# Two tensors in one room of SBUF, 64 or 128 bytes apart: a GNN kernel on one core

## The chip, the core and the metric

The kernel runs on one core of a Trainium2 chip. The metric is the time on the device in microseconds (us) of one execution of the whole program; of several runs the median is given. A profile of one execution shows when each instruction of each engine began and ended.

## The reference

The input x has 64 graphs of 256 nodes with 512 features, in 32-bit floats; adj is one 256 x 256 matrix of zeros and ones that all graphs share. Two layers follow one another, each on a layer norm with a ReLU, and each added to its input:

```python
# layer 0
h = relu(layernorm(x))
q, k, v = h @ Wq.T, h @ Wk.T, h @ Wv.T
rel = adj.T * (q @ k.T)                    # per graph, 256 x 256
rel = rel / norm(rel, axis=2)
x = x + rel @ v
# layer 1
h = relu(layernorm(x))
x = x + (adj @ h) @ weight + bias
```

## The kernel before

The work goes by pairs of graphs: 32 pairs, 512 rows each, one after the other. Since q and k are used only in their product, the kernel works out M = Wq.T Wk once, and per pair g = M h and the scores g.T h. Each 32-bit factor of a product is split into an upper part (u), a lower part (l) and a sum-like third part (s), and three matmuls in a reduced 32-bit format (fp32r) stand for one exact product. So most rooms come as three, named _u, _l and _s.

The stages of a pair that TensorE works on, with the shape of the moving operand:

- g_stage: g = M h, 48 matmuls of 512 columns (stationary m_p, moving h). `split_right_ps` (ACT L265, DVE L266, DVE L268) writes the three parts of g from PSUM into the rooms gy_u, gy_s and gy_l.
- v_stage: v = h Wv, 48 matmuls of 512 columns (stationary h, moving wv_p).
- scores: 48 matmuls of 256 columns. The stationary operand is a 128 x 128 block of g, another one for every matmul; the moving operand is h of one graph, 256 columns.
- attend: rel times v, 24 matmuls of 512 columns.
- gather: adj times the second layer's h, for the pair before, 32 matmuls of 256 columns. The stationary operand is a block of v_low or late_parts, the moving one is the turned adjacency, adjt. `split_left_ps` (ACT L274, DVE L275, L276) writes the three parts of the result, y, into the rooms gy_u, gy_l and gy_s.
- mix: y times the second layer's weight, 48 matmuls of 512 columns (stationary y, moving w_p).

Nearly all matmuls are recorded at one line, L255, the helper `mm`; the profile tells them apart by the names of their operands, the moving one first: `bank<-h_u,gy_u` with 256 columns are scores, `bank<-w_u,gy_u` with 512 are mix, `bank<-adjt_r,late_parts` are gather.

g and y share the three gy rooms in turn: g is written and read by the scores, then y is written and read by mix, then the next pair's g. They don't start at the same byte. A room holds 4 x 512 floats and BEHIND floats more; y starts at its beginning and g BEHIND floats behind:

```python
BEHIND = 16
def as_y(tile):
    return tile[:, : DC * T].rearrange("p (d t) -> p d t", d=DC)
def as_g(tile):
    return tile[:, BEHIND : BEHIND + DC * T].rearrange("p (d t) -> p d t", d=DC)
```

adjt has an offset too: it lies 112 floats (448 bytes) into its room. Rooms are laid out one after the other along each partition, in the order in which they are first declared. Small ones between the large ones (statistics of the layer norms, row norms, two single columns) and the room named level, which nothing uses, set where the large ones begin.

The order of instructions on each engine isn't written out by hand. A planner (`Plan`) takes each step with its engine, an assumed cost and the keys that it reads and writes, simulates the engines, and issues the steps in the order of their simulated starts. Keys are names such as ("gy_u", d, half), not addresses. Because g lies a little behind y, the writing of a block of y also names the end of the block of g that it overlaps, by ("g_u", d - 1, 1) or ("g_u", d, 0).

A program compiled for both cases of the adjacency picks, at run time, the branch for one whose values are exact in the reduced format; this input takes that branch.

Of the kernel before, what the change touches and what calls it, by code (L numbers as in the profile page):

```python
# [113 lines left out]
def kernel(  # L114
# [15 lines left out]
    NC = N // P  # L130
    NB = 2
# [11 lines left out]
    def room(name, *shape, dtype=F32, tag=None):  # L143
        return pool.tile([P, *shape], dtype, name=name, tag=tag or name)

    def parts_room(name, *shape, tag=None):
        return [room(f"{name}_{k}", *shape, dtype=F32R, tag=f"{tag or name}_{k}") for k in "uls"]
# [16 lines left out]

    BEHIND = 16
    w_p = parts_room("w", DC, D)

    def as_y(tile):  # L170
# [5 lines that stand above are left out]
    def norm_rooms(j):  # L176
        return [(room(f"st{j}{n}", TC, 6), room(f"mv{j}{n}", TC, 2), room(f"rs{j}{n}", TC), room(f"nb{j}{n}", TC))
                for n in range(2)]
    wq_room = room("wq_sb", DC * T + BEHIND, tag="gy_u")
    stats = [norm_rooms(0)]  # L180
    norms = [room(f"rn{n}", NB, NC) for n in range(2)]
    wk_room = room("wk_sb", DC * T + BEHIND, tag="gy_l")
    stats.append(norm_rooms(1))
    ones, low_max = room("ones", 1), room("low_max", 1)
    gy_s = room("gy_s", DC * T + BEHIND, dtype=F32R)
    wq_sb, wk_sb = as_y(wq_room), as_y(wk_room)
    low_any = pool.tile([1, 1], I32, name="low_any")
    bias_bc = room("bias_bc", D)
    ident = room("ident", P)
    wq_last, wk_last = room("wq_last", D), room("wk_last", D)  # L190
    room("level", 104)

    rooms = {}

# [427 lines left out]
    def before_pairs():  # L622
        A.activation(norms[1][:, 0, 0:1], ones, AF.Sqrt)
        for _ in range(8):
            mm(bank[7][:, :P], warm, warm, True)
        V.tensor_single_scalar(low, adj_low[:, 0].bitcast(I32), 0xFFF, op=ALU.bitwise_and)
        V.tensor_reduce(low_max, low, axis=mybir.AxisListType.X, op=ALU.max)
        m_products(0)
        mm(bank[7][0:1, 0:1], low_max, ones, True)
        V.tensor_copy(low_any, bank[7][0:1, 0:1])  # L630
        for m in range(NC):
            for n in range(NC):
                nc.tensor.transpose(bank[6][:, ts(m * NC + n, P)], adj_sb[:, n, ts(m, P)], ident)
        for e in range(1, DC - 1):
            m_products(e)
        plan = Plan()
        h_rows(plan, 0, ring[0], "x0")
        plan.run()

    with tc.manual_schedule(engines=in_order):  # L640
        before_pairs()
    gy = [*(room(f"gy_{k}", DC * T + BEHIND, dtype=F32R) for k in "ul"), gy_s]
    g_p, y_p = [as_g(part) for part in gy], [as_y(part) for part in gy]
# [152 lines left out]
```

## Time and profile before

| what | value |
|---|---|
| median of 3 runs | 1561.38 us (1560.41 to 1562.69) |
| the profiled execution's own time | 1560.76 us |
| its span, first to last instruction | 1559.0 us |
| TensorE matmuls | 8046, busy for 1548.2 us |
| TensorE weight loads | busy for 1323.5 us |
| DVE, ACT, GpSimd busy | 1355.3, 1022.7 and 24.3 us |
| granted TensorE clock | 0.999 |

PE in the profile is TensorE's matmuls and PEld its weight loads, which overlap them. A matmul's length in the profile runs from its start to its modelled end, and the next one starts before that end; so the pace is read from one start to the next. In a line of the timeline stand the start in us from the span's start, the length of the merged piece, the engine, the line, the operation, output<-inputs, the shape, and how many instructions were merged.

### The profile page before, as it was taken

What the parts mean: (1) busy time and instruction counts of PE and PEld (TensorE: products, weight loads), DVE (VectorE), ACT (ScalarE), POOL (GpSimd) and SP (SyncE); (2) the same over time, 40 slices, a digit from 0 to 9 for tenths busy, and PEclk for the clock granted to TensorE, in tenths of its full rate; (3) what the DMA queues carried; (4) which work ended last, traced back from release to release, by engine and by line L of the source; (5) the groups of instructions that cost most, each with busy time, mean ns of one, the idle gap of its engine ahead of it and who ended that gap; (6) DMA issues with size and microseconds to landing.
All of it is one profiled execution on the core that took longest, in us unless ns stands there. A gap on an engine that the chain in (4) does not pass through costs nothing.

```text
span 1559.0 us, 22543 instructions
## 1 busy us (share of the span) xinstructions
PE 1548.2 (99%) x8046; PEld 1323.5 (85%) x8046; DVE 1355.3 (87%) x2419; ACT 1022.7 (66%) x1941; POOL 24.3 (2%) x39
## 2 busy tenths in 40 slices
PE   9999999999999999999999999999999999999998
PEld 6788888888888888888888888888888888888886
DVE  6997889898889988898988899888989888989786
ACT  5567666666667676666676675766666766666654
POOL 0000000000000000000000000000000000000000
PEclk9999999999999999999999999999999999999999
DMA  5321333223333223333233332233332233322211
GB/s 199 112 83 41 122 111 120 77 71 110 118 113 119 66 78 117 114 117 90 72 96 118 112 122 68 77 114 114 116 106 71 81 121 111 120 71 76 85 55 56
DMA packets 91112, 153.63 MB, mean 99 GB/s; under 512 B 17136, under 2 KB 32240, under 8 KB 90992
## 3 DMA queue, kind: packets, MB, share of 16 engines
q1 hardware_dynamic: 80768, 116.46, 24.7%
q0 software_dynamic: 8432, 32.51, 5.7%
q10 hardware_dynamic: 1792, 3.15, 0.6%
q8 instruction: 65, 1.06, 0.3%
q14 instruction: 55, 0.45, 0.1%
HBM read 70.78 MB, written 33.55 MB: 67 GB/s over the span
## 4 chain that ended last, share of the span: by engine, by line
PE 95%; DVE 3%; DMA 1%; ACT 0%; issue 0%; ACTq 0%; DVEq 0%
PE bank L255 95%; DMA bias_bc<-in_L_gnn_bias_dram 1%; DMA x_ring<-in_x_dram 1%; DVE late_parts L266 0%; DVE late_parts L268 0%; DVE rel_s_parts L470 0%; DVE st L292 0%; DVE rel_l L475 0%; DVE gy_l L275 0%; DVE m_l L268 0%; DVE gy_l L268 0%; DVE wv_l L268 0%; DVE ht L322 0%; DVE wv_s L266 0%; DVE m_s L266 0%
## 5 line engine op out<-in xcount | busy, mean ns | idle before, releaser
L361 ACT ACTIVATE bank<-bank 128x512 f32<-128x512 f32 x572 | 333.5, 583 | 307.8 <-PE bank L255 304.2
L255 PE MATMUL bank<-wv_s,hs 128*128 128x512 f32 x512 | 137.8, 391 | 0.0
L255 PE MATMUL bank<-wv_u,h_u 128*128 128x512 f32 x512 | 137.5, 390 | 0.0
L255 PE MATMUL bank<-wv_l,h_l 128*128 128x512 f32 x512 | 136.9, 389 | 0.0
L255 PE MATMUL bank<-w_u,gy_u 128*128 128x512 f32 x512 | 136.9, 389 | 0.0
L255 PE MATMUL bank<-w_l,gy_l 128*128 128x512 f32 x512 | 136.9, 389 | 0.0
L255 PE MATMUL bank<-h_l,m_l 128*128 128x512 f32 x512 | 136.6, 389 | 0.1
L255 PE MATMUL bank<-w_s,gy_s 128*128 128x512 f32 x512 | 136.7, 389 | 0.0
L255 PE MATMUL bank<-h_u,m_u 128*128 128x512 f32 x512 | 136.5, 389 | 0.0
L255 PE MATMUL bank<-hs,m_s 128*128 128x512 f32 x512 | 136.4, 389 | 0.0
L266 DVE SCALAR_TENSOR_TENSOR gy_s<-gy_u,bank 128x512 fp32r<-128x512 f32 x128 | 86.2, 675 | 43.0 <-ACT gy_u L265 43.0
L255 PEld LDWEIGHTS bank<-h_l,m_l 128*128 128x128 f32 x512 | 96.0, 188 | 20.4 <-DVE h_l L339 0.5
L255 PEld LDWEIGHTS bank<-wv_l,h_l 128*128 128x128 f32 x512 | 96.1, 188 | 20.2
L255 PEld LDWEIGHTS bank<-h_u,m_u 128*128 128x128 f32 x512 | 96.0, 188 | 20.2 <-ACT m_u L265 0.2
L255 PEld LDWEIGHTS bank<-w_l,gy_l 128*128 128x128 f32 x512 | 96.1, 188 | 20.0
L255 PEld LDWEIGHTS bank<-hs,m_s 128*128 128x128 f32 x512 | 96.1, 188 | 19.9
L255 PEld LDWEIGHTS bank<-w_u,gy_u 128*128 128x128 f32 x512 | 96.0, 188 | 20.0
L255 PEld LDWEIGHTS bank<-w_s,gy_s 128*128 128x128 f32 x512 | 96.0, 188 | 20.0 <-ACT bank L361 0.2
L255 PE MATMUL bank<-adjt_r,late_parts 128*128 128x256 f32 x896 | 112.6, 277 | 0.0
L255 PEld LDWEIGHTS bank<-wv_s,hs 128*128 128x128 f32 x512 | 93.8, 188 | 18.3 <-ACT bank L361 0.7
L255 PEld LDWEIGHTS bank<-wv_u,h_u 128*128 128x128 f32 x512 | 93.7, 188 | 17.7
L255 PEld LDWEIGHTS bank<-adjt_r,late_parts 128*128 128x128 f32 x896 | 107.3, 188 | 0.0
(110 smaller groups left out, 3072.3 us busy)
## 6 DMA issues: line engine op xcount, KB each, us to landing
fresh<-in_x_dram SPq DMA_DIRECT2D x31, 1024.0 KB, 5.7
blocks<-h_rel SPq DMA_DIRECT2D x496, 64.0 KB, 2.0
x_ring<-in_x_dram SPq DMA_DIRECT2D x31, 1024.0 KB, 8.0
out_dram<-x_ring POOLq DMA_DIRECT2D x31, 1024.0 KB, 5.4
h_rel<-h_rel SPq DMA_DIRECT2D x464, 32.0 KB, 1.8
blocks<-in_L_gnn_Wv_dram ACTq DMA_DIRECT2D x1, 1024.0 KB, 11.1
x_ring<-in_L_gnn_weight_dram SPq DMA_DIRECT2D x1, 1024.0 KB, 12.3
out_dram<-x_ring SPq DMA_DIRECT2D x4, 256.0 KB, 2.3
```

Source lines behind the costliest of these rows:

```text
L255: nc.tensor.matmul(out, left, right, start=first, stop=True, skip_group_check=True)
L266: plan.add("DVE", 0.63, lambda: V.scalar_tensor_tensor(s(), f(u()), ONE, ps, op0=ALU.mult, op1=ALU.subtract), [*key, *ku], ks)
L361: plan.add("ACT", 0.49, lambda: A.activation(ps, ps, AF.Copy, scale=ONE), [], [key])
```

## The change

BEHIND goes from 16 to 32 floats, so that g starts 128 bytes behind y in place of 64, and each of the three gy rooms is 64 bytes longer. The small rooms rn0, rn1, ones and low_max, which lay between the large ones, are declared behind the third of them; with that the three gy rooms begin where they began. level shrinks by 48 floats, so that the rooms after it begin where they began. low_any, bias_bc, ident, wq_last and wk_last lie 192 bytes further on.

```diff
-    BEHIND = 16
+    BEHIND = 32
...
     wq_room = room("wq_sb", DC * T + BEHIND, tag="gy_u")
     stats = [norm_rooms(0)]
-    norms = [room(f"rn{n}", NB, NC) for n in range(2)]
     wk_room = room("wk_sb", DC * T + BEHIND, tag="gy_l")
     stats.append(norm_rooms(1))
-    ones, low_max = room("ones", 1), room("low_max", 1)
     gy_s = room("gy_s", DC * T + BEHIND, dtype=F32R)
     wq_sb, wk_sb = as_y(wq_room), as_y(wk_room)
+    norms = [room(f"rn{n}", NB, NC) for n in range(2)]
+    ones, low_max = room("ones", 1), room("low_max", 1)
     low_any = pool.tile([1, 1], I32, name="low_any")
     bias_bc = room("bias_bc", D)
     ident = room("ident", P)
     wq_last, wk_last = room("wq_last", D), room("wk_last", D)
-    room("level", 104)
+    room("level", 56)
```

## The prediction

> **What bounds the kernel now.** I read the profile page first (busy shares, then the chain that ended last), then TensorE's waits, then TensorE's instructions in order of time. The page:
>
> ```profile
> span 1559.0 us, 22543 instructions
> PE 1548.2 (99%) x8046; PEld 1323.5 (85%) x8046; DVE 1355.3 (87%) x2419; ACT 1022.7 (66%) x1941; POOL 24.3 (2%) x39
> PEclk9999999999999999999999999999999999999999
> PE 95%; DVE 3%; DMA 1%; ACT 0%; issue 0%; ACTq 0%; DVEq 0%
> ```
>
> TensorE carries 95% of the chain at an undisturbed clock, and its waits name five single instances that sum to 4.6 us. So the time is the sum of TensorE's own pitches, from one matmul's start to the next one's. A busy time can't show a pitch, because matmuls overlap in the pipeline; starts in the timeline can. One pair in the middle, TensorE alone (start, length, what, how many):
>
> ```profile
> 556.64 1.09 PE L255 MATMUL bank<-wv_s,hs 128*128 128x512 f32 x4
> 557.57 1.11 PE L255 MATMUL bank<-h_u,gy_u 128*128 128x256 f32 x8
> 558.51 1.10 PE L255 MATMUL bank<-h_l,gy_l 128*128 128x256 f32 x8
> 559.45 1.11 PE L255 MATMUL bank<-hs,gy_s 128*128 128x256 f32 x8
> 560.39 0.40 PE L255 MATMUL bank<-adjt_r,v_low 128*128 128x256 f32 x2
> ...
> 562.50 2.66 PE L255 MATMUL bank<-adjt_r,late_parts 128*128 128x256 f32 x22
> 565.00 1.08 PE L255 MATMUL bank<-wv_u,h_u 128*128 128x512 f32 x4
> ```
>
> The scores (moving h, stationary g) take 560.39 - 557.57 = 2.82 us for 24, 117.5 ns each; over all instances the trace gives 117.7. The gather, of the same shape (moving adjt, stationary late rows), takes 2.50 us for 22, 113.6 ns, and 113.3 once settled. A 512-column matmul takes 226.7 ns in steady state, just twice 113.3. So the scores pay 4.4 ns each above a floor that their own shape reaches elsewhere. No engine is waited for, and the clock is the same. Now an early pair:
>
> ```profile
> 130.60 1.07 PE L255 MATMUL bank<-h_u,gy_u 128*128 128x256 f32 x8
> 131.50 1.07 PE L255 MATMUL bank<-h_l,gy_l 128*128 128x256 f32 x8
> 132.41 1.07 PE L255 MATMUL bank<-hs,gy_s 128*128 128x256 f32 x8
> 133.32 0.40 PE L255 MATMUL bank<-adjt_r,v_low 128*128 128x256 f32 x2
> ```
>
> Here the same 24 score matmuls at the same addresses take 2.72 us, 113.3 ns, and the gather that follows in this pair is the slow one, at 118 ns. So there is something like a step between TensorE's two operand streams that persists over hundreds of matmuls, is re-drawn by a disturbance (a 512-column matmul that took 260 ns came just before this pair), and suits either the scores or the gather. Nearly all pairs are of the first kind.
>
> **The addresses.** Laid out from the declared sizes, small rooms rounded up to 32 bytes, and taken modulo 512 bytes: every large room, and so every moving operand of the scores and of all 512-column groups, starts at 128; so do y and nearly all other stationary blocks; adjt starts at 64; g at 192. Scores are thus stationary 192 over moving 128 (64 ahead), the gather 128 over 64 (64 ahead too), everything else 128 over 128. After the change g is at 256, 128 ahead of its moving operand; y does not move, since 64 bytes more of room replace the 64 bytes of small rooms that stood between.
>
> **The change part by part.** No instruction is added, removed or reordered, and no wait: the hand-made schedule works from costs and keys, which are untouched, and y and g overlap in the same blocks as before (the spill of one block into the next grows from 16 to 32 columns of 512, within the same half).
>
> The writes of g (ACT L265, DVE L266 and L268, 128 each) land 64 bytes further. DVE takes 675 ns for gy_s against 668 for the same form into the late rows, which lie at 128: an address costs it under 10 ns, 384 x 10 ns = 3.8 us at most over the span. TensorE hides that: it waits for these engines 2.5 us in all. If that cover were gone, the 3.8 us would be the price. I take 0. The small rooms, bias_bc (L354, 589 ns x128), ident (44 transposes) and wq_last/wk_last (8 matmuls) also move, the four by 192 bytes: the same offset within 64, few or hidden instructions, 0.
>
> What is left is 32 pairs x 48 = 1536 score matmuls with their stationary loads, all on the chain: each ns of their pitch is 1.536 us. No steady stretch of the trace has a stationary 128 bytes ahead, so I bound it. From below: the floor, 113.3 ns, saves 4.4 x 1536 = 6.8 us. Below that no 256-column matmul goes. From above: the second gather matmul after a score block, the slowest that recurs, takes 121.7 ns: 4.0 x 1536 = 6.1 us more. The nearest rows are single matmuls at a border between groups:
>
> ```profile
> 561.21 0.42 PEld L255 LDWEIGHTS bank<-hs,gy_s 128*128 128x128 f32 x3
> 561.33 0.40 PE L255 MATMUL bank<-hs,gy_s 128*128 128x256 f32 x2
> ...
> 564.89 0.77 PEld L255 LDWEIGHTS bank<-wv_u,h_u 128*128 128x128 f32 x4
> 565.00 1.08 PE L255 MATMUL bank<-wv_u,h_u 128*128 128x512 f32 x4
> ```
>
> A load begins some 3 ns behind the matmul under which it runs, so load to next matmul is a pitch. Above, a gather matmul (moving 64) runs while a g block at 192 is loaded, which is 128 ahead: 0.12 us, 117.3 ns as the mean over such borders. Below, the same kind of matmul runs over a load that is 64 ahead, and keeps 113.3 ns. So 128 ahead costs the gather 4.0 ns that 64 ahead does not. The last score matmul before a 512-column group (0 ahead) takes 120.0 ns, against 117.5 for its neighbours, so leaving 64 ahead costs the scores too. Two readings: 128 ahead always gives 117.3 (-0.4 ns, -0.6 us), or it adds its 4.0 to what the scores pay (121.7 ns, +6.1 us). I take 120.0 ns, the score row that has left 64 ahead, between them: 2.3 x 1536 = +3.5 us.
>
> Each score block is followed by a few matmuls that come back into step (556.64 to 557.57: 0.93 us for four where steady ones take 0.907). At some 0.02 us a border and three borders a pair this is 2 us in all; I keep it, between losing most of it (-1.5) and doubling it (+2).
>
> The Trainium skill speaks against any effect: TensorE: Matmul & The Clock Gate, in its step-by-step of a matmul, holds that the two SBUF read ports of TensorE are independent and that loading the next weights takes no bandwidth from the running matmul. By that rule the change is worth 0, 1561.4 us; but it leaves no room for one shape at 113.3 and at 117.7 ns in the same program, so the rows decide.
>
> Sum: the profiled execution took 1560.76 us, its span and 1.76 us around it; with +3.5 it is 1564.3. The median of the runs is 0.62 above the profiled one: 1564.9 us.
>
> **The rivals.** (1) The scores fall into step: 1554 us. Stationary starts at 128 (gather, 512-column groups) all reach the floor in the usual pairs, and only g, at an odd multiple of 64, doesn't. If evenness is what counts, g at 256 joins them: -6.8 us, and with part of the borders gone -7.4. Against it: with stationary and moving both even, the border row has 120.0, and the one row at 128 ahead left the floor. It decides if the step at which the 512-column groups settle is also one for 128 ahead. (2) No change, 1561 us: out of step is out of step, whatever the distance; the pitch stays within 2 ns of 117.7. For it: scores and slow gather have the same 117.8. (3) Worse than my forecast: the new distance also throws the 512-column groups out of step. After the early pair's slow gather, nine of them took 224 to 236 ns, 0.045 us more than nine steady ones; once more in each of 32 pairs that is 1.4 us, and with scores at 121 ns (+5.1 us) the time is near 1568. (4) The change doesn't do what it says, g not moving relative to h: the sizes exclude it, 32 columns of 4 bytes.
>
> **How the numbers follow.** About 0.2%, 3.1 us, is what a measurement of this kernel tells from no change. Slower by more than that: my forecast with rival 3, 0.46. Within: 0.24, rival 2 and the lower part of my own bounds. Faster: rival 1, 0.30. Cases of both signs hold most of the chance, so the likeliest one's own range is 1563 to 1568. The whole range has to reach rival 1: 1553.6 to 1568.2.
>
> **What would show it.** In the changed profile the score groups' starts in the timeline: 24 in 2.88 us if I am right, 2.72 in rival 1, 2.82 in rival 2. The first four 512-column matmuls after a score block show rival 3: over 0.95 us. The gather's 2.50 us for 22, the DVE rows and TensorE's waits should stay. I am wrong if scores keep to 113.3 ns in most pairs, or if TensorE waits anew.

## The result and the profile after

The changed kernel takes 1563.93 us (median of 19 runs, 1563.26 to 1564.79), the kernel before 1561.67 us in its 19 runs beside it (1560.41 to 1562.75). The ratio is 1.0015, 95% interval [1.0008, 1.0021]: slower by 2.3 us, with an interval of 1.2 to 3.3 us. That is a real loss, but a smaller one than the 0.2% that the prediction named as its bound. The profiled execution took 1564.79 us.

The page of the changed kernel, span, busy times, granted clock and the chain that ended last:

```profile
span 1562.9 us, 22543 instructions
PE 1549.8 (99%) x8046; PEld 1325.2 (85%) x8046; DVE 1356.0 (87%) x2419; ACT 1022.7 (65%) x1941; POOL 24.4 (2%) x39
PEclk9999999999999999999999999999999999999999
PE 92%; DVE 4%; ACT 1%; SPq 1%; DMA 0%; issue 0%; DVEq 0%; ACTq 0%
```

The number of instructions is the same, the clock is full, and TensorE is still the bound. Its four longest waits (in all, times, longest):

```profile
PE bank L255 <- DMA wk_sb<-in_L_gnn_Wk_dram: 1.9, 1, 1.9
PE bank L695 <- DVE h_l L662: 1.4, 1, 1.4
PE bank L255 <- DVE rel_s_parts L470: 1.2, 1, 1.2
PE bank L255 <- POOL h_rel L612: 1.0, 1, 1.0
```

These are single waits as before. The two new numbers at the top belong to the start-up, which as a whole is 0.2 us longer (26.4 us before the first matmul of the pairs, now 26.6). So the loss has to lie in the pitch of the matmuls. The timeline of the pair that answers to the one shown of before:

```profile
558.44 1.09 PE L255 MATMUL bank<-wv_s,hs 128*128 128x512 f32 x4
559.37 1.13 PE L255 MATMUL bank<-h_u,gy_u 128*128 128x256 f32 x8
560.33 1.12 PE L255 MATMUL bank<-h_l,gy_l 128*128 128x256 f32 x8
561.29 1.13 PE L255 MATMUL bank<-hs,gy_s 128*128 128x256 f32 x8
562.25 0.39 PE L255 MATMUL bank<-adjt_r,v_low 128*128 128x256 f32 x2
...
563.16 1.11 PE L255 MATMUL bank<-hs,gy_s 128*128 128x256 f32 x8
...
564.34 2.67 PE L255 MATMUL bank<-adjt_r,late_parts 128*128 128x256 f32 x22
566.85 0.39 PE L255 MATMUL bank<-wv_u,h_u 128*128 128x512 f32 x1
```

Read the starts. The 24 scores take 562.25 - 559.37 = 2.88 us, 120.0 ns each, where they took 2.82. The gather's 22 take 566.85 - 564.34 = 2.51 us, as before (2.50). The four 512-column matmuls ahead of the scores take 0.93 us, as before.

Summed from start to start over the whole trace, the two profiled executions stand to each other like this (us; 1536 scores, 1024 gather matmuls; wv_s are the 512-column matmuls with the third part of h, some of which lie beside the score blocks):

| group | before | after | difference |
|---|---|---|---|
| scores | 180.8 | 184.4 | +3.6 |
| gather | 117.6 | 117.0 | -0.6 |
| wv_s | 117.0 | 117.6 | +0.6 |
| all other matmuls | 1110.9 | 1110.9 | 0.0 |
| start-up and end | 32.6 | 33.1 | +0.4 |

Each column is one execution. The +0.6 of wv_s isn't a sure effect of the change: of the runs below, small_rooms, with g at its old distance, has 117.3 us there, and g_384_behind, whose scores go like the changed kernel's, has 117.2.

### The profile page after: what moved, and what is told of

It is laid out like the page before. It is cut to its first block, busy times and chain, and to the rows that moved or that the text cites. A ratio compares the mean times of both kernels' runs of the same rounds, so it can differ in the third digit from the quotient of the medians.

```text
span 1562.9 us, 22543 instructions
## 1 busy us (share of the span) xinstructions
PE 1549.8 (99%) x8046; PEld 1325.2 (85%) x8046; DVE 1356.0 (87%) x2419; ACT 1022.7 (65%) x1941; POOL 24.4 (2%) x39
## 4 chain that ended last, share of the span: by engine, by line
PE 92%; DVE 4%; ACT 1%; SPq 1%; DMA 0%; issue 0%; DVEq 0%; ACTq 0%
PE bank L255 92%; SPq L231 1%; DMA fresh<-in_x_dram 0%; DVE st L292 0%; DVE late_parts L266 0%; DVE gy_l L268 0%; DVE late_parts L268 0%; DVE h_rel L444 0%; ACT h_rel L306 0%; DVE gy_s L266 0%; DVE rel_s_parts L470 0%; DVE gy_l L275 0%; DVE rel_l L475 0%; DVE m_l L268 0%; DVE wv_l L268 0%
## 5 line engine op out<-in xcount | busy, mean ns | idle before, releaser
L255 PE MATMUL bank<-wv_s,hs 128*128 128x512 f32 x512 | 138.4, 392 | 0.1
L255 PE MATMUL bank<-wv_u,h_u 128*128 128x512 f32 x512 | 137.5, 390 | 0.0
L255 PE MATMUL bank<-w_u,gy_u 128*128 128x512 f32 x512 | 136.9, 389 | 0.0
L255 PE MATMUL bank<-wv_l,h_l 128*128 128x512 f32 x512 | 136.9, 389 | 0.0
L255 PE MATMUL bank<-w_l,gy_l 128*128 128x512 f32 x512 | 136.9, 389 | 0.0
L255 PE MATMUL bank<-w_s,gy_s 128*128 128x512 f32 x512 | 136.8, 389 | 0.0
L255 PE MATMUL bank<-h_l,m_l 128*128 128x512 f32 x512 | 136.6, 389 | 0.1
L255 PE MATMUL bank<-h_u,m_u 128*128 128x512 f32 x512 | 136.5, 389 | 0.0
L255 PE MATMUL bank<-hs,m_s 128*128 128x512 f32 x512 | 136.4, 389 | 0.0
L255 PEld LDWEIGHTS bank<-h_l,m_l 128*128 128x128 f32 x512 | 96.0, 188 | 20.4 <-DVE h_l L339 0.5
L255 PEld LDWEIGHTS bank<-wv_l,h_l 128*128 128x128 f32 x512 | 96.1, 188 | 20.1
L255 PEld LDWEIGHTS bank<-h_u,m_u 128*128 128x128 f32 x512 | 96.0, 188 | 20.2 <-ACT m_u L265 0.2
L255 PEld LDWEIGHTS bank<-w_l,gy_l 128*128 128x128 f32 x512 | 96.1, 188 | 20.0
L255 PEld LDWEIGHTS bank<-hs,m_s 128*128 128x128 f32 x512 | 96.1, 188 | 19.9
L255 PEld LDWEIGHTS bank<-w_u,gy_u 128*128 128x128 f32 x512 | 96.0, 188 | 20.0
L255 PEld LDWEIGHTS bank<-w_s,gy_s 128*128 128x128 f32 x512 | 96.0, 188 | 20.0 <-ACT bank L361 0.2
L255 PE MATMUL bank<-adjt_r,late_parts 128*128 128x256 f32 x896 | 112.6, 277 | 0.0
L255 PEld LDWEIGHTS bank<-wv_s,hs 128*128 128x128 f32 x512 | 93.3, 188 | 19.2 <-ACT bank L361 1.8
L255 PEld LDWEIGHTS bank<-wv_u,h_u 128*128 128x128 f32 x512 | 93.7, 188 | 17.7
L255 PEld LDWEIGHTS bank<-adjt_r,late_parts 128*128 128x128 f32 x896 | 106.9, 188 | 0.0
```

The lines of the kernel that those rows point to most:

```text
L255: nc.tensor.matmul(out, left, right, start=first, stop=True, skip_group_check=True)
```

## The experiments

What was in dispute: is it the distance between the starts of a score's two operands (stationary g, moving h) that sets the pitch, the place of the stationary operand by itself, or something about the moved small rooms? And how does the pitch depend on the distance? "Before" is run beside each kernel; its median is 1561.26 us beside small_rooms, g_0_behind, adjt_128 and h64_g128, 1561.05 beside the four at 192 to 448, and 1561.81 beside g_32_behind, g_96_behind, h64_g192 and third_192. "In step" is short for a 256-column group that runs at its floor of 113.3 ns. Sums and means of the scores are taken from start to start over one trace. Pads that keep the other rooms where they were add two lines or more above `mm`, so L255 becomes L256 to L259.

### small_rooms: the new order alone

```diff
 # the changed kernel, but
-    BEHIND = 32
+    BEHIND = 16
+    room("pad_u", 16)   # behind stats of gy_u, and pad_l behind those of gy_l
...
-    room("level", 56)
+    room("level", 72)
```

> g lies 64 bytes behind y as before; only the small rooms, bias_bc, ident, wq_last and wk_last are moved (96 columns' worth of bytes at most), with two unused rooms of 64 bytes in the gaps. If the step between g and its moving operand makes the difference, nothing changes: scores at 117.7 ns from start to start, the time within 0.1% of the kernel before. If the other moved rooms make it, the time is that of the changed kernel, 2.3 us more, with scores still at 117.7 ns and the loss in DVE or ACT rows or in TensorE's waits.

Measured: 1561.72 us, ratio 1.0002 [0.9993, 1.0011]; scores 181.2 us, 118.0 ns each. (Of the 0.4 us more than in the kernel before, some 0.3 lie in one block of 16 scores at 132 ns and one of 8 at 130, each met once; the others run at 117 to 118 in the main.) The new order of the small rooms costs nothing that can be measured. What is lost is lost by the 64 bytes of g.

### g_0_behind, g_192_behind, g_256_behind, g_384_behind, g_448_behind: the distance alone

Each is small_rooms with another BEHIND and pads to match, so that only g's start moves (from 192 on, the large rooms behind the three gy rooms move by 1024 bytes; for 384 and 448 the statistics stand behind the large rooms):

```diff
-    BEHIND = 16
+    BEHIND = 0      # and 48, 64, 96, 112
```

> g and y start at the same byte, so g starts at 128 modulo 512 over a moving operand at 128, distance 0. If the distance between the stationary and the moving start sets the pitch, it gets a pitch of its own; the border row of the kernel before says 120.0 ns, +3.5 us. If what counts is only where the stationary operand starts, and 128 is good since the gather's and the 512-column groups' start there, scores fall to 113.3 ns, -6.8 us. If even against odd multiples of 64 count, the pitch is that of the changed kernel, 120.0 ns.

> g 192 bytes behind y in place of 64, pads of 64 bytes keep every other room's offset in 512 bytes; one ns of score pitch is 1.536 us. So far the scores' mean pitch is 119.3 ns at distance 0, 117.7 at 64, 120.0 at 128 (before: 1561.3 us). Parity theory (only the distance modulo 128 counts): as at 64, 117.7 ns, 1561.3 us. Nearness theory (the two streams of TensorE hinder each other when they read close together, so cyclic distances of 0 to 128 are bad and far ones good): 113.3 ns, 1554.5 us. No-pattern theory (any distance but 64 is as 128): 120 ns, 1564 us.

> g 256 bytes behind y, half of the 512 that one stationary block takes: the farthest that two starts can be apart. Parity theory: as at 0 and 128, 119.3 to 120 ns, 1563.6 to 1564.6 us. Nearness theory: 113.3 ns, 1554.5 us, the best of all distances. No-pattern theory: 120 ns, 1564 us.

> g 384 bytes behind y, which modulo 512 is 128 ahead of its moving operand counted the other way (128 before it). Parity theory: 119.3 to 120 ns, 1563.6 to 1564.6 us. Nearness theory, if only the cyclic distance counts: as at 128, 120 ns, 1564 us; if order counts (who runs ahead of whom), anything from 113.3 (1554.5 us) on. No-pattern theory: 120 ns, 1564 us.

> g 448 bytes behind y, modulo 512 that is 64 before its moving operand, the mirror image of the kernel before. Parity theory and cyclic nearness theory: as at 64, 117.7 ns, 1561.3 us. If order counts, that is if the scores' two streams are apart by the distance less a fixed lead, the time differs from that at 64: 113.3 ns and 1554.5 us if 64 before the moving operand is clear of it, 120 ns and 1564 us if it is not. No-pattern theory: 120 ns, 1564 us.

| g behind its moving operand | scores, us | mean, ns | median, us | ratio to before |
|---|---|---|---|---|
| 0 | 183.2 | 119.3 | 1563.55 | 1.0014 [1.0005, 1.0023] |
| 64 (small_rooms) | 181.2 | 118.0 | 1561.72 | 1.0002 [0.9993, 1.0011] |
| 128 (the change) | 184.4 | 120.0 | 1563.93 | 1.0015 [1.0008, 1.0021] |
| 192 | 180.9 | 117.8 | 1561.65 | 1.0003 [0.9994, 1.0012] |
| 256 | 182.9 | 119.1 | 1563.04 | 1.0010 [1.0001, 1.0019] |
| 384 | 184.2 | 119.9 | 1563.89 | 1.0020 [1.0011, 1.0029] |
| 448 | 180.9 | 117.8 | 1561.58 | 1.0003 [0.9994, 1.0012] |

(The column counts from h's start at 128 modulo 512, where y starts as well.) The timelines show it in one pair each. First line the start of the 24 scores, last line the start of what follows; 256 behind, 2.87 us:

```profile
559.16 1.11 PE L257 MATMUL bank<-h_u,gy_u 128*128 128x256 f32 x8
...
562.03 0.40 PE L257 MATMUL bank<-adjt_r,v_low 128*128 128x256 f32 x2
```

384 behind, 2.88 us, what the change shows:

```profile
558.70 1.13 PE L256 MATMUL bank<-h_u,gy_u 128*128 128x256 f32 x8
...
561.58 0.39 PE L256 MATMUL bank<-adjt_r,v_low 128*128 128x256 f32 x2
```

448 behind, 2.82 us, what the kernel before shows:

```profile
558.12 1.10 PE L256 MATMUL bank<-h_u,gy_u 128*128 128x256 f32 x8
...
560.94 0.40 PE L256 MATMUL bank<-adjt_r,v_low 128*128 128x256 f32 x2
```

The parity theory (only the distance modulo 128 counts) fits these times, the nearness theory falls: 256, the farthest apart, is no better than 0, and at none of these distances does the scores' mean come near 113.3 ns. The traces say more than parity. The sequences of single pitches are alike, within 1 ns, at 0 and 256 (settling at 120, 120, 120), at 128 and 384 (120, 122 or 123, 117 or 118, over and over; the mean is again 120), and at 192 and 448 (117.8, with 115, 117, 117, 118 ns from the last score of the block of 24 on, where 64 has 117, 121, 122, 116). So, with h where it is, the distance counts modulo 256 bytes in the three pairs that were run; 320, the partner of 64, was not. Odd multiples of 64 cost 117.8 ns, even ones some 120 once settled.

### g_32_behind and g_96_behind: between the steps

```diff
-    BEHIND = 16
+    BEHIND = 8      # and 24
```

> g 32 bytes behind y, half way between 0 (scores 119.3 ns, 1563.6 us) and 64 (117.7 ns, 1561.3 us); every other room keeps its offset in 512 bytes. The runs so far gave one pattern for 0 and 256, one for 128 and 384, one for 192 and 448, so the distance counts modulo 256, in what looks like four steps of 64. Steps theory (bytes are read 64 at a time, and a start inside a step counts as that step's): 119.3 ns or 117.7 ns, 1561.3 to 1563.6 us. Fine theory (the distance acts continuously): between or beyond the two; from 113.3 ns (1554.5 us) if 64 bytes are just past a good place, to over 120 ns (over 1564 us) if a block that starts inside a step costs one read more.

> g 96 bytes behind y, half way between 64 (117.7 ns, 1561.3 us) and 128 (120.0 ns, 1564 us). Steps theory: 117.7 or 120.0 ns, 1561.3 to 1564 us. Fine theory: between or beyond the two, 1554.5 us at the best, over 1564 us if a start inside a step costs a read more.

Measured: 1562.21 us, ratio 1.0003 [0.9994, 1.0012], scores 118.4 ns; and 1562.64 us, ratio 1.0004 [0.9995, 1.0013], scores 118.2 ns. Both times are no different from before by the interval. Both mean pitches lie between those of the neighbours, though that of g_96_behind is only 0.2 ns above small_rooms, less than two executions at one distance differ (117.7 and 118.0). The single pitches tell more: they run from 115 to 123 ns and keep to no single value (in g_96_behind's blocks of 24 they repeat over five matmuls, 120, 116, 117, 119, 122), and at neither distance is the sequence that of a neighbour. The steps theory falls. The fine one fits in its plain form, between the two neighbours; no start inside a step was better than 64.

### adjt_128: another group of the same shape

If the distance does it, a gather whose stationary blocks start 128 bytes ahead of the moving operand, as the scores' do in the changed kernel, has to get slower too.

```diff
 # small_rooms, and
-        adjt[:] = [turned_adj[:, P - 16 : P - 16 + NC * N].rearrange("p (c n) -> p c n", c=NC)]
+        adjt[:] = [turned_adj[:, P - 32 : P - 32 + NC * N].rearrange("p (c n) -> p c n", c=NC)]
```

> g lies 64 bytes behind y as before, but adjt starts 64 bytes earlier in its room, so that the gather's stationary blocks are 128 ahead of the moving operand, as the scores' are in the changed kernel; the scores stay. If the distance sets the pitch, the gather goes from 114.9 ns over all its matmuls to about 120, 1024 x 5 = 5 us more, near 1567. If only the stationary's own start counts, the gather stays at 114.9 ns and the time at 1561.7.

Measured: 1564.56 us, ratio 1.0023 [1.0013, 1.0033], with g as before. The gather in the timeline:

```profile
563.80 2.78 PE L257 MATMUL bank<-adjt_r,late_parts 128*128 128x256 f32 x22
566.41 1.09 PE L257 MATMUL bank<-wv_u,h_u 128*128 128x512 f32 x4
```

22 matmuls take 2.61 us, 118.6 ns each, in place of 2.50; the gather's sum goes from 117.6 to 121.6 us, 4.0 and not 5 more, and the scores' from 180.8 to 180.0. So the effect isn't g's alone: this second group of 256 columns has it, and moving the other operand brings it about as well. But the same distance of 128 settles at 120.0 ns for the scores of the changed kernel (256 over 128) and at 118.7 here (128 over 0; pitches of 120, 119, 115, 117, 122, over and over). So the distance isn't the whole answer.

What ran before counts too. The eight scores between the two gather groups of a pair fall into step here in 30 of 32 pairs (117, 116, 114, then 113 ns), at their own distance of 64, which didn't change; with adjt where it was they stay near 117.5. And in the changed kernel the same eight scores, behind the gather, go by 119, 113, 117, 123, 120, 119, 115 ns, much as the long gather group begins here (121, 112, 117, 123, 120, 119, 115), while the blocks of 24 there go by 120, 123, 117. So one distance, 128, has two sequences in one kernel.

### h64_g128 and h64_g192: both operands moved

h goes to 64 modulo 512, all three parts; g to 128 and to 192. The distances are 64 and 128 as before and after, at other places.

```diff
+    room("pad_h", 112)
     h = [room(f"h_{k}", DC, T, dtype=F32R) for k in "ul"]
+    room("pad_h2", 16)   # and the third part 64 bytes lower than a multiple
...
-    BEHIND = 16
+    BEHIND = 0           # h64_g192: 16
```

> h (all three parts) starts at 64 modulo 512 and g at 128, with y and g at the same byte: the scores' operands lie just as the gather's do in the kernel before, 128 over 64. If the distance alone counted, this would be like 192 over 128: 117.7 ns and 1561.7 us. If the absolute places count too, the scores do what the gather does, 113.3 ns after a few matmuls: up to 6.8 us less, 1555. The 512-column groups change as well: g_stage then has 128 over 64, v_stage 64 over 128; if these leave their 226.7 ns, each ns there costs 1.5 us a stage.

> h (u, l and the third part) at 64 modulo 512 and g at 192: 128 apart as in the changed kernel, but both at odd multiples of 64. As in h64_g128 the 512-column groups lie 64 apart from their other operand and pay for that, so it is compared with h64_g128 (1570.9 us, scores 177.3 us in all). Distance theory: the scores take what they take in the changed kernel, 184.4 us, so 1578 us. Theory of the stationary's own place (odd multiples of 64 give 117.7 ns whatever moves): 180.8 us, so 1574.4 us. The changed kernel's own reading of evenness (odd both, so as good as even both) is no different from the distance theory here.

Measured: 1570.94 us, ratio 1.0060 [1.0047, 1.0074], and 1575.59 us, ratio 1.0088 [1.0074, 1.0102]. The timeline of h64_g128, a 512-column group and the scores of the same pair:

```profile
552.38 1.10 PE L259 MATMUL bank<-hs,m_s 128*128 128x512 f32 x4
553.31 1.10 PE L259 MATMUL bank<-wv_u,h_u 128*128 128x512 f32 x4
...
561.69 1.09 PE L259 MATMUL bank<-h_u,gy_u 128*128 128x256 f32 x8
562.62 1.07 PE L259 MATMUL bank<-h_l,gy_l 128*128 128x256 f32 x8
563.52 1.07 PE L259 MATMUL bank<-hs,gy_s 128*128 128x256 f32 x8
564.43 0.39 PE L259 MATMUL bank<-adjt_r,v_low 128*128 128x256 f32 x2
```

Two things are to be seen. The 512-column group takes 0.93 us for four, 233 ns each, in place of 0.907: these groups ran at their floor of 226.7 ns at distance 0, and h at 64 sets them 64 apart. Over the trace the groups with h take 713.5 us in place of 698.7, and that is more than the whole loss. And the scores, still 64 apart, fall into step here: the 24 take 564.43 - 561.69 = 2.74 us, with 113.3 ns from the fourth on, while the 16 ahead of them stay at 117.8 (each in 30 of 32 pairs). Their sum is 177.3 us, 3.5 less than before.

At distance 128 (h64_g192) the scores take 182.0 us, 4.7 more than at 64 in the same places; the two times differ by 4.65 us, or by 4.1 when each is taken against the kernel before in its own session (9.7 and 13.8 us). The distance theory wanted +7.1, the theory of the stationary's own place +3.5. Neither has the number: 128 apart is dearer than 64 apart here as well, but the pitches settle at a mean of 118.7, in the sequence of adjt_128's gather, and not at 120.

### third_192: an attempt at a version that beats both

The traces showed the gather, with its moving operand 64 bytes lower than what ran before it, coming into step where scores didn't. So I tried to put the scores into that position.

```diff
-    m_p, wv_p = (parts_room(w, DC, D) for w in ("m", "wv"))
+    m_p, wv_p = ([room(f"{w}_{k}", DC, D, dtype=F32R) for k in "ul"] for w in ("m", "wv"))
+    room("pad_third", 16)
+    for w, parts in (("m", m_p), ("wv", wv_p)):
+        parts.append(room(f"{w}_s", DC, D, dtype=F32R))
+    room("pad_after", 112)
...
-    g_p, y_p = [as_g(part) for part in gy], [as_y(part) for part in gy]
+    g_p, y_p = [as_g(part, b * BEHIND) for part, b in zip(gy, (1, 1, 2))], [as_y(part) for part in gy]
```

> The third parts alone (m_s, wv_s, the third part of h) move from 128 to 192 modulo 512, and g's third part with them to 256, so that every pair of operands keeps its distance (512-column groups 0, scores 64). Phase theory: the gather falls in step behind out-of-step scores because its moving operand starts 64 bytes lower than theirs; a score block's first parts follow a group of third parts, which now starts 64 bytes higher than they do, so h_u and h_l scores fall in step too: 1024 x 4.4 ns less, 4.5 us, and 1556.8 us; every group of 512-column third parts costs two shifts of phase, up to 1.7 us in all if each pair of shifts costs a full 6.7 ns, so 1556.8 to 1558.5 us. Distance theory alone (only the pair's own distance counts, not what came before): no change, 1561.3 us, or up to 1563 us with the shifts.

Measured: 1562.76 us, ratio 1.0008 [0.9999, 1.0017]. The timeline of a pair:

```profile
554.72 1.09 PE L259 MATMUL bank<-wv_s,hs 128*128 128x512 f32 x4
555.65 1.09 PE L259 MATMUL bank<-h_u,gy_u 128*128 128x256 f32 x8
556.57 1.07 PE L259 MATMUL bank<-h_l,gy_l 128*128 128x256 f32 x8
557.48 1.08 PE L259 MATMUL bank<-wv_s,hs 128*128 128x512 f32 x4
558.40 1.10 PE L259 MATMUL bank<-h_u,gy_u 128*128 128x256 f32 x8
559.34 1.11 PE L259 MATMUL bank<-h_l,gy_l 128*128 128x256 f32 x8
560.29 1.08 PE L259 MATMUL bank<-hs,gy_s 128*128 128x256 f32 x8
```

The first 16 scores do fall in step: 557.48 - 555.65 = 1.83 us, 114.4 ns each, where 117.8 stood. The next 16, behind a group of the same third parts, don't (560.29 - 558.40 = 1.89 us, 118 ns). So half of the phase theory's effect is there and half is not, and the theory as stated falls: which state a group enters isn't given by the start of the group ahead alone. The scores save 2.1 us in all; the gather gives back 0.4, and the 512-column matmuls of the third parts give back 1.9 (m_s) and 1.6 us (wv_s). That this is the price of their new place against their neighbours was not tested by itself. No version that I ran beats the kernel before.

## Why the prediction was right, and where it was off

- **The bound.** TensorE's pitch is the bound: the scores' sum moved by 3.6 us, and no other row of the table by more than 0.6.
- **Terms taken as nothing.** The new order of the small rooms is worth nothing (small_rooms). The writes of g are too; the DVE row of gy_s in the changed page, at 676 ns, was 675:

```profile
L266 DVE SCALAR_TENSOR_TENSOR gy_s<-gy_u,bank 128x512 fp32r<-128x512 f32 x128 | 86.3, 676 | 43.0 <-ACT gy_u L265 43.0
```

- **The scores' term.** 120.0 ns and +3.5 us were forecast; the trace has 120.0 ns and +3.6 us. The number was right, the reason that chose it only in part. It came from the last score matmul before a 512-column group, which "has left 64 ahead": the load that runs under it is at distance 0. For distance 0 that row was a good guide: g_0_behind settles at 120.0. That 128 has the same mean, by another sequence, no row of the prediction showed, so in this the forecast had luck. The one row at 128 ahead, the gather's 117.3, was a poor guide: adjt_128's gather, at that distance throughout, settles at 118.7. And "left 64 ahead" isn't the reason, since scores at 192 and 448 have left 64 too and stay at 117.8. What fits all seven distances is that 128 is an even multiple of 64 and 64 an odd one. That is rival 1's evenness turned round: even is the bad case for 256 columns, though the 512-column groups were better at distance 0 than at 64.
- **The borders: the term that was mis-sized.** I kept the 2 us of borders, between -1.5 and +2. The gather behind the scores now comes into step sooner: its first eight take 563.16 - 562.25 = 0.91 us in place of 561.33 - 560.39 = 0.94, and its sum falls by 0.6 us; g_384_behind repeats that (117.0). It does not repeat the +0.6 of wv_s, so I leave that out. With the gather the ledger gives +3.0 us for scores and gather, inside the interval of 1.2 to 3.3, where 3.5 is just outside.
- **From one execution to the median.** The forecast of 1564.9 us is 1.0 too high: its loss of 3.5 us is 1.2 above the measured 2.3, and its base, the median of three runs, is 0.3 below that of 19. Of the 1.2 the gather is 0.6. The other 0.6 isn't traced to a group, and it may be the choice of executions: the two profiled ones are 4.0 us apart and not 2.3, because that of before lies 0.91 us below its median and that of after 0.86 above. g_384_behind, with the same pitches in its scores and its gather as the change, has a span of 1561.6 us, 1.3 less than the change; that much a single execution may be off. Two executions of each kind (before and small_rooms; the change and g_384_behind) put scores and gather together at +2.7 us on the mean. The time lies in the likeliest case's own range, 1563 to 1568, but the loss of 0.15% is below the 0.2% from which that case was counted as slower, and so falls among the outcomes that had 0.24.
- **Rival 1** (in step, 1554 us) is excluded: with h where it is, no distance brought the scores' mean near 113.3 ns (the nearest, 117.8, is at odd multiples of 64). Even the early pair of before that had its scores in step has lost it; in the changed timeline the 24 take 2.85 us:

```profile
130.82 1.12 PE L255 MATMUL bank<-h_u,gy_u 128*128 128x256 f32 x8
...
133.67 0.40 PE L255 MATMUL bank<-adjt_r,v_low 128*128 128x256 f32 x2
```

- **Rival 2** (out of step is out of step) fails at 128 (120.0 ns, more than 2 ns above 117.7), and would have been right at 192 or 448. **Rival 3** (512-column groups thrown out too) asked for over 0.95 us for four behind the scores, and 0.93 was found; the sum of all 512-column groups but wv_s moved by 0.1 us.
- **The Trainium skill's rule.** TensorE: Matmul & The Clock Gate, in its step-by-step of a matmul, has two independent read ports and no loss from loading the next weights. By that alone all of these distances would take the same time. The scores' sums disagree by 3.0 us between 64 (small_rooms, 181.2) and 384 (184.2), with the same instructions; the measurement decides. The runs don't show whether it is the load that holds the matmul up or the other way round.

What stays open is the mechanism within TensorE's two streams: why even multiples of 64 are the bad ones, and why one distance has several settled pitches, depending on what ran before.

## What to carry to other kernels

When TensorE is the bound, read the pitch of each group from starts, not from busy times, and compare groups of one shape: where nothing is waited for and the clock is full, a difference between them may come from the addresses of the operands, as it did here. Then scan one operand's start in steps of 64 bytes over 256 by padding one room; here 2.3 us of 1561 lay between the best distances and the worst, and the pads of small_rooms cost nothing that could be measured. Don't move a room that several groups share for the sake of one of them: h at 64 helped the scores by 3.5 us and cost the 512-column groups 14.8.

## What the runs showed of the hardware

- The settled pitch of a 256-column fp32r matmul, as a mean over its repeating sequence, took one of a few values at a granted clock of 0.999 to 1.000: 113.3 ns (gather 64 apart; scores 64 apart in h64_g128), 117.8 (scores 64, 192 or 448 apart), 118.7 (gather 128 apart in adjt_128; scores 128 apart in h64_g192), 120.0 (scores 0, 128, 256 or 384 apart with h at 128).
- With h at 128, the distance between the two operands' starts counted modulo 256 bytes: the sequences of single pitches were alike within 1 ns at 0 and 256, at 128 and 384, and at 192 and 448.
- 512-column matmuls took 226.7 ns at distance 0 and up to 233 ns at 64 (h64_g128), the opposite order to the 256-column scores.
- Groups keep or lose their step by what ran before them: at one and the same distance of 64, the first 16 scores of a pair stayed at 117.8 ns in h64_g128 and the next 24 fell to 113.3.
